# Interleaving the first two units of a down projection over shared weight tiles

## The chip, the cores and the metric

The kernel runs on one core of a Trainium2 chip. The metric is device time in microseconds, the median of three runs. A core has TensorE (PE, with its weight loads shown as PEld), VectorE (DVE), ScalarE (ACT), GpSimd (POOL) and SyncE (SP); here SP issues every transfer.

## The reference

One transformer block over 4096 tokens of width 512, all in float32: causal linear attention, a residual and a layer norm, then a feed-forward network and a second residual and layer norm. The change lies in the last part of the feed-forward network:

```
x = fwht(x * SU_ug) / SCALE
x_up   = x @ W_up.T   * (Wscale_ug[:INTER] * SCALE)      # INTER = 2048
x_gate = x @ W_gate.T * (Wscale_ug[INTER:] * SCALE)
x = silu(x_gate) * x_up
x = fwht(x * SU_dp) / SCALE
x = x @ W_down.T * (Wscale_dp * SCALE)                   # 2048 -> 512: the down projection
x = layernorm(residual + x)
```

The second transform and the scales are folded into W_down ahead of time.

## The kernel before

The kernel goes through its work in stages: attention, output projection, gate/up, down. The gate/up stage has 32 rounds `n` (four blocks `f` of 1024 tokens by eight `p`). It stores its results to DRAM (`hop_d`). The down stage takes them up again as eight units `(f, jp)` of 512 tokens.

Both stages multiply 2 x 2 block matrices with seven products instead of eight. So a unit of the down stage has seven products `s` from 0 to 6. Product `s` multiplies an operand of the unit (activations, or sums of them, from `hop_d`) with weight matrix `s` (from `wdop_d`), and the results are added up in PSUM and on VectorE. `SEQ` names the PSUM bank of each product: a, c, a, b, a, a, b. In the profile these banks are `ps_da`, `ps_dc` and `ps_db`.

Each operand is float32 and is cut into a high and a low part by `hilo`: ScalarE copies it into the high part (L89), and VectorE or GpSimd subtracts (L90). Each multiplication then takes three matmuls (high by high, high by low, low by high). One product of a unit is 48 matmuls of 128 x 256.

The names and lines that matter:
- `h_load(n, s)` loads the operand of unit `n`, product `s`, in four quarters (`hraw`) of 256 KB. `h_split` cuts them into `hah` and `hal`. `h_split_x` does it for the first two operands, into other memory (`hxh`, `hxl`).
- `load_b(s)` loads weight matrix `s` in four quarters (`braw`) of 256 KB. `split_b(s)` cuts them into `wdh`, `wdl` (quarters 0 and 1) and `wdzh`, `wdzl` (quarters 2 and 3), kept in `BW[s]` for all units.
- `hraw` and `braw` share the pool `rp` of 10 buffers: a new load waits until an older quarter has been cut. `hah` and `hal` share 19 buffers.
- `y_load(n)` loads the residual rows of unit `n` as two halves (`yres`). There are two buffers for each half. `acc` (L1035, in the changed file L1034) adds a bank to `yres`. `finish` normalizes a half and stores it to `out`.
- The products of the last round of gate/up (`cc` L882 and L852, `sg` L891, sums `hS` L942) are stored to `hop_d` while the down stage begins.

The list `order` says in which order the products run. Units 0 to 7 run one after the other, with product 0 of each next unit moved ahead of product 5 of the one before:

```
order = [(n, s) for n in range(len(units)) for s in range(7)]
for n in range(1, len(units)):
    order.remove((n, 0))
    order.insert(order.index((n - 1, 5)), (n, 0))
```

During unit 0 every product also cuts one weight matrix and loads another, and the last round of gate/up already prepares the operands of products 0 and 1 and weights 0 to 2. From unit 1 on, only activations are loaded.

The program order is not the final order. The framework's scheduler (`schedule_with_timeline_sim=True`) sets the order of the instructions on each engine, from its own estimate of times. On the chip each engine then runs its list in order, and an instruction that waits holds up all behind it. SP is such a list too.

Of the kernel before, what the change touches and what calls it, by code (L numbers as in the profile page):

```python
# [43 lines left out]
def kernel(  # L44
# [734 lines left out]
    HR, HOP, YN, bank = {}, {}, {}, {}  # L779
    units = [(f, jp) for f in range(4) for jp in range(2)]  # L780

    def h_load(n, s):
        f, jp = units[n]
        HR[n, s] = []
        for qd in range(4):
            raw = rp.tile([128, 2, 256], F32, tag="ar", name="hraw")
            dma(raw, hop_d[f][s, jp, :, 2 * qd:2 * qd + 2])
            HR[n, s].append(raw)

    def load_b(s):  # L790
        RAW["b", s] = []
        for j in range(4):
            x = rp.tile([128, 2, 256], F32, tag="ar", name="braw")
            dma(x, wdop_d[s][:, 2 * j:2 * j + 2])
            RAW["b", s].append(x)
# [13 lines left out]
            ops[l] += [hl[l][:, r] for r in range(4)]  # L809
        BW[s] = ops  # L810

    def h_split_x(s, his, los):
        HOP[0, s] = []
        for qd, raw in enumerate(HR.pop((0, s))):
            hi, lo = (x[qd // 2][:, 2 * (qd % 2):2 * (qd % 2) + 2] for x in (his, los))
            hilo(hi, lo, raw, G if qd == 3 else V)
            HOP[0, s].append((hi, lo))

    with ExitStack() as es:
        pa = es.enter_context(tc.tile_pool(name="g1", bufs=1, reuse_waits="tile"))  # L820

        def utile(name):
            return pa.tile([128, 512], F32, tag="u", name=name, bufs=16)

        def araw(name):
            return rp.tile([128, 2, 2, 128], F32, tag="ar", name=name)

        def ff_front(i):
            y2 = []
            for e in range(2):  # L830
                y = utile("y_nat")
                dma(y, y_d[2 * i + e])
                y2.append(y)
            yield
            yield from front(i, y2, pa, lambda s, n: pgu.tile(s, F32, tag="a", name=n, bufs=4),
                             lambda s, n: pgu.tile(s, F32, tag="a", name=n, bufs=4), (ytile, xtile))

        for s in range(7):
            aload(1, s, araw("A"))
        NS = 32  # L840
        yraw, late_puts = [], []
        fr = None
        for n in range(NS):
            f, p = divmod(n, 8)
            bank, sv, c = {}, {}, {}

            def emit(u, q, x):
                if u == 1:
                    S.activation(x, x, AF.Silu)  # L849
                    c["g", q] = x  # L850
                else:
                    G.tensor_tensor(x, x, c.pop(("g", q)), ALU.mult)  # L852
                    c["h", q] = x

            if n in (1, 2, 4, 5):
                step(fr, 9)
                fr = ff_front(12 + (1, 2, 4, 5).index(n))
            new = {}
            for s, tag in enumerate(SEQ):
                first = SEQ.index(tag) == s  # L860
                wh, wl = AOP.pop((n, s))
                yh, yl = YOPS[s]
                for u in (1, 0):
                    if first:
                        bank[tag, u] = pgu.tile([128, 512], F32, tag=tag, name="ps_" + tag, bufs=4 if tag == "a" else 2)
                    ps = bank[tag, u]
                    i = 0
                    for k in range(2):
                        for w, y in ((wh, yh), (wh, yl), (wl, yh)):
                            T.matmul(ps, w[:, u, k], y[:, k], start=first and i == 0, stop=i == 5,  # L870
                                     skip_group_check=not first)
                            i += 1
                    it = 2 * p + (s >= 4 and s < 6)
                    sc = wsc[:, u, it:it + 1]
                    if s in (0, 2, 4):
                        x = pa.tile([128, 512], F32, tag="sv", name="sv", bufs=6)
                        S.activation(x, ps, AF.Copy, scale=sc)  # L877
                        sv[s, u] = x
                    if s in (1, 4, 6):
                        src, k, q = {1: (ps, 0, 0), 4: (bank.get(("b", u)), 4, 3), 6: (ps, 2, 1)}[s]  # L880
                        x = utile("cc")
                        V.scalar_tensor_tensor(x, src, sc, sv[k, u], ALU.mult, ALU.add)  # L882
                        emit(u, q, x)
                    if s == 5:
                        if u == 1:
                            x = utile("sg")
                            S.activation(x, ps, AF.Silu, scale=sc)
                            c["g", 2] = x
                        else:
                            x = c.pop(("g", 2))  # L890
                            V.scalar_tensor_tensor(x, ps, sc, x, ALU.mult, ALU.mult)  # L891
                            c["h", 2] = x
                if n and s in (1, 2, 3):
                    for _ in range(3):
                        if late_puts:
                            late_puts.pop(0)()
                if n + 1 < NS:
                    asplit(n + 1, s)
                if n + 2 < NS:
                    aload(n + 2, s, araw("A"))  # L900
                if p == 7:
                    if f < 3:
                        new[s] = ysplit(s, yraw[s])
                        if s < 5:
                            yraw.append(yload(f + 1, s + 2))
                    elif s == 0:
                        hx = [xtile([128, 4, 256], F32R, "hxh") for _ in range(2)]
                        hx += [ytile([128, 4, 256], F32R, x) for x in ("hxl", "hxl", "hxh", "hxh", "hxl", "hxl")]
                        h_split_x(0, hx[0:2], hx[2:4])
                        h_load(0, 1)  # L910
                    elif s == 2:
                        split_b(0)
                        load_b(1)
                    elif s == 3:
                        h_split_x(1, hx[4:6], hx[6:8])
                        load_b(2)
                    elif s == 4:
                        split_b(1)
                        h_load(0, 2)
                    elif s == 6:  # L920
                        split_b(2)
                        load_b(3)
                elif n == NS - 2:
                    if s == 4:
                        h_load(0, 0)
                    elif s == 6:
                        load_b(0)
                step(fr)
            if p == 6 and f < 3:
                yraw = [yload(f + 1, 0), yload(f + 1, 1)]  # L930
            YOPS.update(new)
            H = {"A11": c["h", 0], "A12": c["h", 2], "A21": c["h", 1], "A22": c["h", 3]}

            def put(key, f=f, p=p, H=H):
                dma(hop_d[f][WKEY.index(key)].rearrange("j p i t -> p j i t")[:, :, p],
                    H[key].rearrange("p (j t) -> p j t", j=2))

            late_puts = [lambda k=k, put=put: put(k) for k in ("A11", "A12", "A22", "S1", "S3", "S2", "S4")]
            for key, x0, x1, op in (("S1", "A21", "A22", ALU.add), ("S3", "A11", "A21", ALU.subtract),
                                    ("S2", "S3", "A22", ALU.subtract), ("S4", "A12", "S2", ALU.add)):  # L940
                H[key] = utile("h" + key)
                G.tensor_tensor(H[key], H[x0], H[x1], op)  # L942

    with ExitStack() as es:
        pd = es.enter_context(tc.tile_pool(name="d1", bufs=2, reuse_waits="tile"))
        order = [(n, s) for n in range(len(units)) for s in range(7)]
        for n in range(1, len(units)):
            order.remove((n, 0))
            order.insert(order.index((n - 1, 5)), (n, 0))
        def y_load(n):  # L950
# [38 lines left out]
            dma(out[t * 128:(t + 1) * 128], y)  # L989

        y_load(0)
        for idx, (n, s) in enumerate(order):
            if 0 < idx and idx + 1 < len(order):
                h_split(*order[idx + 1])
            if n == 0 and s + 3 < 7:
                split_b(s + 3)
            if 0 < idx and idx + 2 < len(order):
                h_load(*order[idx + 2])
            if n == 0 and s + 4 < 7:
                load_b(s + 4)  # L1000
            if idx > 0:
                for put in late_puts[:3]:
                    put()
                late_puts = late_puts[3:]
            if s == 3 and n + 1 < len(units):
                y_load(n + 1)
            tag = SEQ[s]
            first = SEQ.index(tag) == s
# [98 lines left out]
```

## Time and profile before

| what | value |
|---|---|
| median of three runs | 2345.06 us (2343.75 to 2345.25) |
| time of the profiled execution | 2340.29 us |
| span of the profiled execution | 2338.2 us |
| granted TensorE clock, mean | 0.989 |
| TensorE (PE) busy | 2269.3 us, 97% |
| VectorE busy | 1812.0 us, 77% |
| ScalarE busy | 1401.7 us, 60% |
| GpSimd busy | 1243.7 us, 53% |
| moved by DMA | 484.16 MB, mean 207 GB/s |
| first matmul of the down stage (L1025) | 1984.75 us |
| last matmul of gate/up (L870) starts | 1999.60 us |

Times in the profile count from the start of the span. A busy engine is not at once the bound: what counts is which wait ends last at a place. "Granted clock" is the share of full speed at which TensorE was let run. In a list of waits, "A <- B" means that A stood idle until B was done.

### The profile page before, as it was taken

To read this page: it belongs to the slowest core of one execution; us is meant where nothing else is said; L and a number is where in the kernel's file an instruction comes from. 1 tells how busy PE (TensorE), PEld (TensorE's weight loads), DVE (VectorE), ACT (ScalarE), POOL (GpSimd) and SP (SyncE) were. 2 spreads that over 40 slices of the span, in tenths; PEclk is the share of its full clock that TensorE was granted. 3 is DMA by queue.
4 is the path that set the end of the run, shared out by engine and by line. 5 is a ranking of instruction groups with operands and counts; after the bars stand their busy time and mean duration, and the time that the engine had idled before them with its cause. 6 is when DMAs were issued, how large, how long until landed. Compare 5 with 4: busy or idle time off the path is not lost.

```text
span 2338.2 us, 42338 instructions
## 1 busy us (share of the span) xinstructions
PE 2269.3 (97%) x14432; PEld 2015.0 (86%) x14432; DVE 1812.0 (77%) x2812; ACT 1401.7 (60%) x2483; POOL 1243.7 (53%) x999
## 2 busy tenths in 40 slices
PE   7999999988999999899999999999999999899998
PEld 6999999987899999688878887788878888799998
DVE  7999999988898889678898776676766766665555
ACT  6777777766677777344444466655655655555553
POOL 2455454476654445367888526565565555533332
PEclk9999999999999999899999999999999999899999
DMA  6554555677744445878997977775765657867673
GB/s 186 145 152 146 161 161 155 170 214 218 213 133 129 129 135 142 279 256 269 279 294 253 312 240 217 245 254 187 227 207 188 223 189 212 285 229 249 224 248 128
DMA packets 369528, 484.16 MB, mean 207 GB/s; under 512 B 68670, under 2 KB 224384, under 8 KB 365344
## 3 DMA queue, kind: packets, MB, share of 16 engines
q1 hardware_dynamic: 369312, 481.45, 66.0%
q8 instruction: 114, 1.87, 0.3%
q14 instruction: 102, 0.84, 0.1%
HBM read 282.76 MB, written 156.76 MB: 188 GB/s over the span
## 4 chain that ended last, share of the span: by engine, by line
PE 83%; DVE 6%; DMA 5%; issue 2%; POOL 2%; ACT 1%; SPq 1%; DVEq 0%; POOLq 0%; ACTq 0%
PE ps_wo L737 15%; PE ps_a L870 15%; PE ps_qk L244 13%; PE ps_da L1025 8%; PE ps_b L870 7%; PE ps_num L371 5%; PE ps_db L1025 4%; PE ps_c L870 4%; PE ps_s L294 3%; PE ps_v L197 3%; PE ps_dc L1025 2%; PE ps_sc L337 1%; PE ps_sc L338 1%; PE ps_den L372 1%; DVE x L230 1%
## 5 line engine op out<-in xcount | busy, mean ns | idle before, releaser
L351 POOL TENSOR_SCALAR_AFFINE_SELECT A<-A 64x512 fp32r<-64x512 f32 x256 | 220.4, 861 | 286.9 <-DVE am L347 187.5
L244 PE MATMUL ps_qk<-xh,wh 128*128 128x256 f32 x1280 | 358.9, 280 | 6.3 <-DVE x L230 3.7
L244 PE MATMUL ps_qk<-xl,wh 128*128 128x256 f32 x1280 | 356.9, 279 | 0.6 <-DVE xl L90 0.6
L244 PE MATMUL ps_qk<-xh,wl 128*128 128x256 f32 x1280 | 357.1, 279 | 0.0
L90 DVE TENSOR_TENSOR wol<-A,woh 128x512 fp32r<-128x512 f32 x217 | 231.4, 1071 | 106.9 <-ACT woh L89 92.4
L852 POOL TENSOR_TENSOR cc<-cc 128x512 f32<-128x512 f32 x96 | 149.2, 1556 | 278.8 <-ACT cc L849 169.9
L226 POOL TENSOR_TENSOR sw<-sw,csb 128x512 f32<-128x512 f32 x160 | 219.7, 1374 | 141.9 <-ACT sw L225 133.8
L244 PEld LDWEIGHTS ps_qk<-xh,wh 128*128 128x128 f32 x1280 | 242.5, 189 | 8.0 <-DVE x L230 3.3
L244 PEld LDWEIGHTS ps_qk<-xl,wh 128*128 128x128 f32 x1280 | 241.7, 189 | 2.0 <-DVE xl L90 0.8
L244 PEld LDWEIGHTS ps_qk<-xh,wl 128*128 128x128 f32 x1280 | 241.7, 189 | 0.8
L89 ACT ACTIVATE woh<-A 128x512 fp32r<-128x512 f32 x217 | 135.5, 630 | 129.0 <-PE ps_b L870 75.2
L89 ACT ACTIVATE hah<-hraw 128x512 fp32r<-128x512 f32 x216 | 134.8, 630 | 129.5 <-PE ps_da L1025 68.1
L870 PE MATMUL ps_a<-yol,woh 128*128 128x512 f32 x512 | 202.5, 395 | 0.0
L90 POOL TENSOR_TENSOR hal<-hraw,hah 128x512 fp32r<-128x512 f32 x77 | 101.5, 1319 | 189.1 <-PE ps_da L1025 73.1
L870 PE MATMUL ps_a<-yoh,woh 128*128 128x512 f32 x512 | 201.9, 396 | 0.0
L870 PE MATMUL ps_a<-yoh,wol 128*128 128x512 f32 x512 | 199.4, 396 | 0.0
L90 DVE TENSOR_TENSOR hal<-hraw,hah 128x512 fp32r<-128x512 f32 x139 | 102.3, 744 | 111.7 <-PE ps_da L1025 45.7
L737 PE MATMUL ps_wo<-wh,oh 128*128 128x512 f32 x448 | 178.6, 399 | 2.8 <-ACT oh L89 2.8
L737 PE MATMUL ps_wo<-wh,ol 128*128 128x512 f32 x448 | 178.6, 399 | 0.0
L737 PE MATMUL ps_wo<-wl,oh 128*128 128x512 f32 x448 | 178.0, 397 | 0.0
L231 ACT ACTIVATE sw<-x,neg 128x512 f32<-128x512 f32 x160 | 115.5, 722 | 78.0 <-DVE x L230 75.9
L877 ACT ACTIVATE sv<-ps_a,wsc 128x512 f32<-128x512 f32 x192 | 127.2, 680 | 39.6 <-PE ps_a L870 39.5
(256 smaller groups left out, 7290.2 us busy)
## 6 DMA issues: line engine op xcount, KB each, us to landing
hraw<-hop_d SPq DMA_DIRECT2D x224, 256.0 KB
vd<-vhl SPq DMA_DIRECT2D x128, 256.0 KB
num_d<-num SPq DMA_DIRECT2D x128, 256.0 KB
rb<-rec_d SPq DMA_DIRECT2D x128, 256.0 KB
hop_d<-hS SPq DMA_DIRECT2D x128, 256.0 KB
nt<-num_d SPq DMA_DIRECT2D x31, 1024.0 KB
A<-in_wug_dram SPq DMA_DIRECT2D x93, 256.0 KB
hop_d<-cc SPq DMA_DIRECT2D x64, 256.0 KB
```

Of the source, the lines that this page charges most:

```text
L89: S.activation(hi, src, AF.Copy)
L90: eng.tensor_tensor(lo, src, hi.bitcast(F32), ALU.subtract)
L226: G.tensor_tensor(sw, sw, sinb, ALU.mult)
L231: S.activation(sw, x1, AF.Exp, bias=neg1)
L244: T.matmul(ps[:, j], W[key][wa][:, k * 128:(k + 1) * 128], B[xa][:, k], start=i == 0, stop=i == 11)
L351: G.affine_select(ah, ah.bitcast(F32), pattern=[[0, 8], [1, 64]], compare_op=ALU.is_ge, fill=0.0, base=0, channel_multiplier=-1)
L371: T.matmul(ps[:, c2], l, r, start=i == 0, stop=i == len(ops) - 1)
L737: T.matmul(ps, l[:, h], r, start=i == 0, stop=i == 47)
L852: G.tensor_tensor(x, x, c.pop(("g", q)), ALU.mult)
L870: T.matmul(ps, w[:, u, k], y[:, k], start=first and i == 0, stop=i == 5, skip_group_check=not first)
L877: S.activation(x, ps, AF.Copy, scale=sc)
L1025: T.matmul(ps[:, j], ops[qd][al][:, r, js], BW[s][bl][ip], start=first and i == 0, stop=i >= 45 or last and i == 23, skip_group_check=True)
```

## The change

Units 0 and 1 take turns: (0,0), (1,0), (0,1), (1,1) and so on to (0,6), (1,6), so that each weight matrix is used twice in a row when it is new. One weight matrix is then cut and one loaded for two products, not for one. Unit 2 starts after (1,6) with all its products in their order; from unit 3 on, the order is the old one.

The preparation in the last round of gate/up changes with it: it loads and cuts the operand of (1,0), in place of (0,1), loads that of (0,1), in place of (0,2), no longer cuts weight 2 and no longer loads weight 3. The residual rows of units 0 and 1 are both loaded at the start, those of unit 2 at (1,6).

```diff
--- before.py
+++ after.py
@@ -809,12 +809,12 @@
             ops[l] += [hl[l][:, r] for r in range(4)]
         BW[s] = ops
 
-    def h_split_x(s, his, los):
-        HOP[0, s] = []
-        for qd, raw in enumerate(HR.pop((0, s))):
+    def h_split_x(n, his, los):
+        HOP[n, 0] = []
+        for qd, raw in enumerate(HR.pop((n, 0))):
             hi, lo = (x[qd // 2][:, 2 * (qd % 2):2 * (qd % 2) + 2] for x in (his, los))
             hilo(hi, lo, raw, G if qd == 3 else V)
-            HOP[0, s].append((hi, lo))
+            HOP[n, 0].append((hi, lo))
 
     with ExitStack() as es:
         pa = es.enter_context(tc.tile_pool(name="g1", bufs=1, reuse_waits="tile"))
@@ -907,7 +907,7 @@
                         hx = [xtile([128, 4, 256], F32R, "hxh") for _ in range(2)]
                         hx += [ytile([128, 4, 256], F32R, x) for x in ("hxl", "hxl", "hxh", "hxh", "hxl", "hxl")]
                         h_split_x(0, hx[0:2], hx[2:4])
-                        h_load(0, 1)
+                        h_load(1, 0)
                     elif s == 2:
                         split_b(0)
                         load_b(1)
@@ -916,10 +916,7 @@
                         load_b(2)
                     elif s == 4:
                         split_b(1)
-                        h_load(0, 2)
-                    elif s == 6:
-                        split_b(2)
-                        load_b(3)
+                        h_load(0, 1)
                 elif n == NS - 2:
                     if s == 4:
                         h_load(0, 0)
@@ -943,8 +940,9 @@
 
     with ExitStack() as es:
         pd = es.enter_context(tc.tile_pool(name="d1", bufs=2, reuse_waits="tile"))
-        order = [(n, s) for n in range(len(units)) for s in range(7)]
-        for n in range(1, len(units)):
+        order = [(n, s) for s in range(7) for n in range(2)]
+        order += [(n, s) for n in range(2, len(units)) for s in range(7)]
+        for n in range(3, len(units)):
             order.remove((n, 0))
             order.insert(order.index((n - 1, 5)), (n, 0))
         def y_load(n):
@@ -989,20 +987,21 @@
             dma(out[t * 128:(t + 1) * 128], y)
 
         y_load(0)
+        y_load(1)
         for idx, (n, s) in enumerate(order):
             if 0 < idx and idx + 1 < len(order):
                 h_split(*order[idx + 1])
-            if n == 0 and s + 3 < 7:
-                split_b(s + 3)
+            if n == 0 and s + 2 < 7:
+                split_b(s + 2)
             if 0 < idx and idx + 2 < len(order):
                 h_load(*order[idx + 2])
-            if n == 0 and s + 4 < 7:
-                load_b(s + 4)
+            if n == 1 and s + 3 < 7:
+                load_b(s + 3)
             if idx > 0:
                 for put in late_puts[:3]:
                     put()
                 late_puts = late_puts[3:]
-            if s == 3 and n + 1 < len(units):
+            if n and s == (6 if n == 1 else 3) and n + 1 < len(units):
                 y_load(n + 1)
             tag = SEQ[s]
             first = SEQ.index(tag) == s
```

## The prediction

> **What bounds the kernel now.** I read the page first, then the chain of waits, the waits of TensorE, and the windows and timelines around the one hole that these showed.
>
> ```profile
> span 2338.2 us, 42338 instructions
> PE 2269.3 (97%) x14432; PEld 2015.0 (86%) x14432; DVE 1812.0 (77%) x2812; ACT 1401.7 (60%) x2483; POOL 1243.7 (53%) x999
> PEclk9999999999999999899999999999999999899999
> ```
>
> TensorE is busy for 97% of the span and runs at full clock but for two of the forty slices. So only a hole in TensorE's row, or a slow clock behind one, can give time. The second of those slices (2280 to 2338) is the tail, which the change leaves alone. The change lies at about 2000 us; TensorE's waits there:
>
> ```profile
> PE ps_da L1025 <- ACT hah L89: 10.5, 1, 10.5
> PE ps_da L1025 <- DVE hal L90: 0.6, 1, 0.6
> ```
>
> One wait of 10.5 us, for a ScalarE split. What ScalarE did (start, duration, idle time before it and its cause):
>
> ```profile
> 2009.27 0.63 ACT L89 ACTIVATE wdh<-braw 128x512 fp32r<-128x512 f32 x1 [6.89 <-DMA braw<-wdop_d]
> 2010.51 0.63 ACT L89 ACTIVATE wdh<-braw 128x512 fp32r<-128x512 f32 x1 [0.61 <-DMA braw<-wdop_d]
> 2015.55 0.63 ACT L89 ACTIVATE wdzh<-braw 128x512 fp32r<-128x512 f32 x1 [4.41 <-DMA braw<-wdop_d]
> 2016.74 0.63 ACT L89 ACTIVATE wdzh<-braw 128x512 fp32r<-128x512 f32 x1 [0.56 <-DMA braw<-wdop_d]
> 2017.28 3.22 ACT L89 ACTIVATE hah<-hraw 128x512 fp32r<-128x512 f32 x6
> ```
>
> The activations (`hah`) that TensorE wants at 2007 stand in ScalarE's queue behind four splits of weight matrix 5, which is needed three products later. Its quarters 2 and 3 load into the buffers that quarters 0 and 1 leave, so two transfers follow each other. The chain of waits prices a transfer of 256 KB, early and late in the hole:
>
> ```profile
> 1986.37 3.05 DMA braw<-wdop_d
> 1997.37 3.34 DMA braw<-wdop_d
> 2005.91 4.58 DMA braw<-wdop_d
> 2012.51 4.21 DMA braw<-wdop_d
> ```
>
> The clock by 4 us windows (last columns: granted clock, DMA share, GB/s):
>
> ```profile
> 2004.00:2008.00 4.00, 3.48 (x30) 3.28 (x28) 1.56 (x3) 0.00 (x0) 2.88 (x3) 1.00 0.86 273
> 2008.00:2012.00 4.00, 0.00 (x0) 0.00 (x0) 1.71 (x2) 1.26 (x2) 3.78 (x3) 0.90 0.86 275
> 2012.00:2016.00 4.00, 0.00 (x0) 0.00 (x0) 1.08 (x2) 0.45 (x1) 0.00 (x0) 0.50 0.94 314
> 2020.00:2024.00 4.00, 4.00 (x21) 4.00 (x21) 4.00 (x3) 2.41 (x5) 3.63 (x3) 0.50 1.02 377
> 2024.00:2028.00 4.00, 4.00 (x32) 4.00 (x32) 4.00 (x6) 2.67 (x6) 1.74 (x1) 0.89 0.99 354
> ```
>
> Mixing 1.00 and 0.50 in these rows, the clock halved at 2011.2, 3.8 us after the last matmul, and came back at 2024.9, 5.5 us after matmuls ran without a break (2019.33).
>
> **What the hole costs.** The next product could have begun at 2007.3 and ended 5.7 us later (48 matmuls take 5.71 us in the chain), at 2013.0. It ended at 2027.3 (first `ps_db` matmul 2027.36). The loss is 14.3 us: 10.6 until its first matmul, 1.1 more until the third (0.6 of it the wait for `hal`), 2.5 from matmuls every 0.21 us and not 0.119.
>
> **Traffic.** In unit 0 every product (5.7 us) needs four loads of activations and four of weights: 2.1 MB, 368 GB/s. The fastest row above moved 377 at a DMA share of 1.02. After the change, two products (11.4 us) share four weight loads: 12 loads, 3.1 MB, 276 GB/s, a rate that the trace holds with room. ScalarE, VectorE and GpSimd likewise split 12 quarters per 11.4 us instead of 16. I cost the later pairs at nothing; the cover is TensorE's own 11.4 us per pair. In the old order TensorE had no wait from 2019.4 to the tail, though DMA moved 338 GB/s from 2020 to 2040.
>
> **The new order, step by step.** Instructions, matmuls and transfers are the same in number; only their order changes, up to the third unit; I read it from the changed program, engine by engine, with what each instruction waits for. Until 1991 the queues agree, so times are on the trace's clock. (u,s) is unit u, product s.
>
> 1. TensorE now runs (0,0), (1,0), then (0,1), (1,1). The last gate/up matmul still ends at 2000, and (1,0) at 2007.4, where the second product ended before. Then (0,1) is wanted.
> 2. ScalarE's queue now has the splits of weight 3 ahead of `hah` of (0,1): the same queue jam, with weight 3 in place of 5, and earlier. Its quarter 0 is issued once VectorE has split quarter 2 of weight 2: about 1994.15. Landing 3.3 us later, 1997.45; `wdh` 0.63, `wdl` 0.69: 1998.8; quarter 2 is issued at 1998.9. Quarter 1 (issued 1996.5, behind a GpSimd split) lands at 1999.8; its `wdl` stands behind `cc` and `sg` on VectorE (0.74 each) and a SiLU on ScalarE: 2001.4. Quarter 3 is issued at 2001.5. With 3.9 us (between 3.34 early and 4.58 late) it lands at 2005.4; its split ends at 2006.0. `hah` of (0,1), quarters 0 and 1: 2006.6 and 2007.1, in time.
> 3. The new wait. On VectorE the `yres` addition of (1,0) stands ahead of every `hal` of (0,1). It needs unit 1's `y` rows, whose loads stand on SP behind quarter 3 and a `hraw` load, issued at 2004.4 and 2004.8; landing 2008.7 at 3.9 us. Addition 0.69 (2009.4), `hal` 0.8 (such splits take 0.68 to 1.78 us in the trace, the most when GpSimd works beside them): 2010.2. TensorE, idle since two matmuls after 2007.4, goes on then: a gap of 2.6 us. Behind that addition wait all VectorE splits, for them TensorE, and on SP the loads that want their buffers.
> 4. GpSimd: `cc` (2003.4), two `hS` of 1.25 (2005.9), `wdzl` of quarter 3 (2007.3), two more `hS` (2009.9), then `hal` of quarter 1: 2011.3; TensorE wants it at 2011.6. No loss.
> 5. `hah` of quarter 2 reuses memory of the gate/up stage and waits for the store of S2 (issued 2008.7, landed 2012.6 at 3.9 us): `hah` 2013.2, `hal` 2013.9, wanted at 2013.0. Gap 0.9 us. Quarter 3 is in time.
> 6. (0,1) ends at 2016.5 where 2013.0 was possible: 3.5 us lost. The loads of (0,2) are issued by about 2014, and TensorE wants them from 2022; each later product has more slack.
> 7. Units 1 to 2: `y` of unit 2 takes unit 0's buffer and waits for its output store. Counting from the end of (0,6): normalized by 7.2 us, stored by 11.3, `y` loaded by 16, added by 18; TensorE asks for it at 20.8, since product (2,3) has been put ahead of (2,2). 2.8 us spare: nothing. From unit 3 the order is the old one.
>
> Gain: 14.3 − 3.5 = 10.8 us. The profiled execution took 2340.29 us (span 2338.2 and 2.1 around it), so it would become 2329.5. It lies 4.8 us (0.2%) below the median of 2345.06; on the median I predict **2334.3**.
>
> **Bounds, and two rules weighed.** *Transfer time.* Every load in the jam lies between 3.05 and 4.7 us (quarter 2 of weight 5, issued 2010.84, used 2015.55). The Trainium skill (DMA: Bandwidth & Descriptors, Anatomy of one DMA) gives 2.0 us plus bytes over 436 GB/s, for another queue: 2.6 us for 256 KB. By it, step 3's gap shrinks to some 1.3 us and step 5's goes: 1.5 lost, gain 12.8. The rows are of this queue under this traffic, so I take them. At 4.7 throughout, the chain of step 2 ends at 2007.6, `y` at 2011.8, the first `hal` at 2013.2: a gap of 5.6 us.
> *Clock.* The row: halved 3.8 us after the last matmul. The skill (TensorE: Matmul & The Clock Gate) speaks against this change: it allows no gap over about 3 us (Why this matters for your kernels), and its window runs free of the kernel (What's actually happening). My 2.6 us gap passes by both; at 3.3 us the rule would halve the clock and the row would not. A halving costs 2.5 us by the row of this trace, 3.0 with the slow first two matmuls. So the loss lies between 0 (all covered) and 5.7 + 3.0 = 8.7 us; I take 3.5.
>
> **The rivals.**
> - *Slow landings and a cold clock* (0.22): the 5.6 us gap and the clock loss, 8.7 us in all. Gain 5.6: 2339.5. For it: 4.2 to 4.7 us was what transfers took at 2005 to 2016. Against: the chain's first half lies before 2002, where they took 3.0 to 3.4.
> - *The hole only moves* (0.11): the change doesn't do what it says, since weight 3 blocks the queue as weight 5 did. The loss is again 13 to 14 us: 2345. For it: the queue order in step 2. Against: weight 3 starts 11 us earlier than weight 5 did (1994.15 against 2005.4).
> - *Slower* (0.08): the jam comes back at weights 4, 5 and 6, whose splits stand before `hah` in ScalarE's queue too. Each such hole would cost 14.3 us; two give 2334.3 + 28.6, about 2363. It decides once these holes sum to over 10.8 us. Against: weight 4 should be split by 2026, and (1,2), behind it, is wanted from 2030.
>
> **How the numbers follow.** The likeliest case, a small gap at full clock, has 0.59; faster than before by over 0.2% (4.7 us, about what a measurement of this kernel can tell from no change) are it and most of the second case (0.18 of 0.22): 0.77. Within 0.2%: 0.15. Slower: 0.08. The range goes from no loss at all (2330.8, less a microsecond of spread: 2329.5) to just past the second case: 2341.0.
>
> **What would show it.** Right: TensorE's longest wait near 2000 falls from 10.5 us to about 3, for `hal` from VectorE rather than `hah`; the granted clock stays at 1.00 there; the `yres` addition of unit 1 ends near 2009; all later matmuls start about 11 us earlier. Wrong: a clock row of 0.5, a wait of ScalarE for `braw` that reaches past 2008, a new TensorE wait in the paired products, or one for `yres` at the third unit.

## The result, and the profile after

The changed kernel takes 2340.89 us (median of 20 runs, 2339.28 to 2348.49) where the kernel before takes 2345.99 in the same series (20 runs, 2342.94 to 2350.96). The ratio is 0.9982, with a 95% interval of 0.9975 to 0.9988: about 4.2 us gained, between 2.8 and 5.9. Forecast were 10.8 us. The sign was right, the size less than half.

The profiled execution has nearly the same span as that of before, so the page alone shows no gain:

```profile
span 2338.0 us, 42331 instructions
PE 2269.2 (97%) x14432; PEld 2015.3 (86%) x14432; DVE 1813.9 (78%) x2811; ACT 1401.8 (60%) x2483; POOL 1250.3 (53%) x1000
PEclk9999999999999999899999999999999999999999
```

The two executions differ ahead of the change: the last gate/up matmul starts at 2004.17 here and at 1999.60 in the profile of before, and the work up to there was not edited but for the last round of gate/up. Compared matmul by matmul, the whole difference is there by 1590 us. Such differences are the spread from run to run (8 to 9 us in either series). Stages must therefore be compared from a common point. From that matmul to the last recorded matmul pass 327.14 us, against 331.93 before: 4.8 us gained, in agreement with the ratio.

A ledger of that stretch tells more. Matmuls of the down stage follow each other every 0.1189 us; what a stretch takes beyond its count times 0.1189 is lost. Before, 14.3 us are lost at the hole, and 1.9 in the tail, which is the same in every trace to 0.1 us and left out below. After the change 8.1 us are lost at the same place, and 1.3 at the third unit: 9.4 in all.

TensorE's waits after the change (total, times, longest):

```profile
PE ps_dc L1024 <- DVE hal L90: 3.4, 1, 3.4
PE ps_dc L1024 <- ACT hah L89: 2.0, 1, 2.0
PE ps_da L1024 <- DVE yres L1034: 1.9, 2, 1.1
```

The wait of 10.5 us has become one of 2.0 for `hah` and one of 3.4 for `hal`, with two matmuls between them; of the third row, 1.06 us are new (0.88 is the tail's). ScalarE's timeline shows why `hah` is late (start, duration, idle before and its cause):

```profile
2004.14 0.64 ACT L89 ACTIVATE wdh<-braw 128x512 fp32r<-128x512 f32 x1 [3.79 <-DMA braw<-wdop_d]
...
2008.85 0.63 ACT L89 ACTIVATE wdzh<-braw 128x512 fp32r<-128x512 f32 x1 [1.45 <-DMA braw<-wdop_d]
2012.97 0.63 ACT L89 ACTIVATE wdzh<-braw 128x512 fp32r<-128x512 f32 x1 [3.48 <-DMA braw<-wdop_d]
2013.50 1.14 ACT L89 ACTIVATE hah<-hraw 128x512 fp32r<-128x512 f32 x2
```

It is the picture of before with weight 3 in place of weight 5: four splits, three of them (shown) waiting for transfers, and behind them the activations that TensorE wanted at 2012.2. On VectorE the same queue holds up the end of gate/up (the `wdl` stands ahead of `cc` and `sg`), and the residual addition of unit 1 stands ahead of every `hal`:

```profile
2004.81 0.69 DVE L90 TENSOR_TENSOR wdl<-braw,wdh 128x512 fp32r<-128x512 f32 x1 [5.84 <-ACT wdh L89]
2016.60 0.69 DVE L1034 TENSOR_TENSOR yres<-ps_da,yres 128x512 f32<-128x512 f32 x1 [5.22 <-DMA yres<-y_d]
2017.21 0.86 DVE L90 TENSOR_TENSOR hal<-hraw,hah 128x512 fp32r<-128x512 f32 x1
```

And the clock was halved again. The windows (TensorE's busy time first; granted clock, DMA share and GB/s last):

```profile
2012.00:2016.00 4.00, 0.68 (x4) 0.30 (x2) 0.00 (x0) 1.67 (x3) 3.48 (x3) 1.00 0.79 234
2016.00:2020.00 4.00, 1.88 (x9) 1.89 (x10) 1.47 (x2) 0.08 (x1) 3.11 (x3) 0.52 0.94 303
2020.00:2024.00 4.00, 4.00 (x24) 4.00 (x24) 3.07 (x3) 4.00 (x8) 2.85 (x2) 0.63 1.00 280
```

Of the 8.1 us, 5.9 are the gap and 2.2 the matmuls at half clock that follow it.

### The profile page after: what moved, and what is told of

Read it like the earlier page. It is cut to its first block, busy times and chain, and to the rows that moved or that the text cites. A ratio compares the mean times of both kernels' runs of the same rounds, so it can differ in the third digit from the quotient of the medians.

```text
span 2338.0 us, 42331 instructions
## 1 busy us (share of the span) xinstructions
PE 2269.2 (97%) x14432; PEld 2015.3 (86%) x14432; DVE 1813.9 (78%) x2811; ACT 1401.8 (60%) x2483; POOL 1250.3 (53%) x1000
## 4 chain that ended last, share of the span: by engine, by line
PE 81%; DVE 7%; DMA 6%; issue 2%; POOL 2%; ACT 1%; SPq 1%; DVEq 0%; POOLq 0%; ACTq 0%
PE ps_wo L737 15%; PE ps_a L870 14%; PE ps_qk L244 13%; PE ps_b L870 7%; PE ps_da L1024 7%; PE ps_num L371 5%; PE ps_db L1024 4%; PE ps_c L870 4%; PE ps_s L294 3%; PE ps_v L197 3%; PE ps_dc L1024 2%; PE ps_sc L337 1%; PE ps_den L372 1%; PE ps_sc L338 1%; DVE x L230 1%
## 5 line engine op out<-in xcount | busy, mean ns | idle before, releaser
L90 POOL TENSOR_TENSOR hal<-hraw,hah 128x512 fp32r<-128x512 f32 x78 | 106.4, 1368 | 178.0 <-PE ps_da L1024 73.5
L90 DVE TENSOR_TENSOR hal<-hraw,hah 128x512 fp32r<-128x512 f32 x138 | 108.1, 791 | 94.2 <-PE ps_da L1024 37.8
```

What stands on the lines that cost most here:

```text
L90: eng.tensor_tensor(lo, src, hi.bitcast(F32), ALU.subtract)
```

## The experiments

All ratios are to the kernel before, from runs on the same chip. The ledger gives what one profiled execution lost (us, tail left out).

| kernel | lost at the first hole | lost later | ratio, 95% interval |
|---|---|---|---|
| before | 14.3 | 0 | 1 |
| the change | 8.1 | 1.3 | 0.9982 (0.9975 to 0.9988) |
| the change again | 7.5 | 4.3 | 0.9983 (0.9975 to 0.9991) |
| weights 3 to 6 later | 1.9 | 13.8 | 0.9978 (0.9970 to 0.9987) |
| y halves exchanged | 6.4 | 3.7 | 0.9972 (0.9961 to 0.9983) |
| useless matmuls in the gap | 7.8 | 5.8 | 0.9980 (0.9972 to 0.9987) |
| old order, late weights | 9.3 | 2.7 | 0.9986 (0.9979 to 0.9993) |
| unit 0 ended first | 6.3 | 0.6 | 0.9975 (0.9965 to 0.9985) |
| pairs, old prefetch | 10.0 | 1.7 | 0.9991 (0.9985 to 0.9998) |
| three repairs | 0.4 | 6.8 | 0.9965 (0.9952 to 0.9977) |
| three repairs again | 0.4 | 5.8 | 0.9957 (0.9943 to 0.9972) |
| three repairs, other boundary | 0.4 | 5.7 | 0.9954 (0.9942 to 0.9966) |

The profiled executions of "weights 3 to 6 later" and "useless matmuls" were 3 to 4 us slower than the medians of their kernels (spans of 2342.7 and 2343.1 us), so their later losses are probably on the high side. In the first of them the trace lost 15.7 us in all, more than the kernel before, although the ratio says 5 us faster. One trace gives the place of a loss; only the ratios give the size. The intervals of the single edits overlap with that of the change, so none of them alone is shown to be faster or slower than it. In the row of the useless matmuls, the 3.8 us of useless work count as lost.

**Which half of the change gives the gain?** The change does two things: it pairs the products (with both units' residual rows loaded at the start), and it takes up weights one product later. First the later weights alone, in the old order:

```
-            if n == 0 and s + 3 < 7:
-                split_b(s + 3)
+            if n == 0 and s + 2 < 7:
+                split_b(s + 2)
...
-            if n == 0 and s + 4 < 7:
-                load_b(s + 4)
+            if n == 0 and s + 3 < 7:
+                load_b(s + 3)
```

(and without the split of 2 and the load of 3 in the last gate/up round).

> The old order of products (no interleaving) with the change's later prefetch alone: weight s+2 is split and weight s+3 is loaded in each product of unit 0, and the last gate/up round no longer splits 2 and loads 3. Theory A (the place of the queue jam decides, the interleaving little): weight 4 stands in the jam, earlier than weight 5 did; hole 6.5 to 7.5 us instead of 10.5, halved clock, loss about 10 us against 14.3 of the old order, so 4 us faster than it, near to the change itself. Theory D (interleaving is what gives the gain): no faster than the old order, or slower through new waits of TensorE for weights in products 3 to 6 of unit 0.

It gained 3.3 us. ScalarE's splits in the jam are now those of weight 4:

```profile
2009.90 0.63 ACT L89 ACTIVATE wdh<-braw 128x512 fp32r<-128x512 f32 x1 [5.73 <-DMA braw<-wdop_d]
2010.75 0.64 ACT L89 ACTIVATE wdh<-braw 128x512 fp32r<-128x512 f32 x1 [0.21 <-DMA braw<-wdop_d]
2015.17 0.63 ACT L89 ACTIVATE wdzh<-braw 128x512 fp32r<-128x512 f32 x1 [3.78 <-DMA braw<-wdop_d]
2017.92 0.63 ACT L89 ACTIVATE wdzh<-braw 128x512 fp32r<-128x512 f32 x1 [2.12 <-DMA braw<-wdop_d]
2018.45 1.13 ACT L89 ACTIVATE hah<-hraw 128x512 fp32r<-128x512 f32 x2
```

The hole costs 9.3 us, as theory A had it, and the small new waits (2.7 us lost before products 4 and 5 of unit 0, where theory D had looked for them) don't eat the gain.

Then the pairs alone, with the old prefetch (`split_b(s + 3)`, `load_b(s + 4)`, and the split of 2 and the load of 3 in the last round again).

> The changed order of products with the old order's prefetch: weights 2 and 3 are taken up in the last gate/up round, weight s+3 is split and s+4 loaded in the pairs. Weight 4 then stands in the jam. With the experiment before it (old order, late prefetch: about 9.3 us lost at the hole) this is the other half of the change alone. Theory A (the place of the jam decides): a hole of 6 to 7 us and a halved clock, loss 9 to 10 us, 3 to 5 us faster than the old order. Theory D (the interleaving is the gain): loss 8 us or less, as in the change.

10.0 us at the hole, weight 4 in the jam again, a gain of 2.1 us (0.5 to 3.5). Theory D fails in both. Each half moves the jam from weight 5 to weight 4, the two together to weight 3. With each step it begins earlier and costs less: the first split of the jam starts 9.7 us after the last gate/up matmul before, 5.0 and 4.9 us after it with one half, and together with it in the change. The size fell a little below what theory A gave, because 1.7 us went at the third unit.

**What holds the gap of the change open?** Weight 3 was taken out of the jam, the pairs kept. Against the words of the expectation below, the edit takes up weights 4 to 6 one product later too:

```
-            if n == 0 and s + 2 < 7:
-                split_b(s + 2)
+            if n == 0 and s == 0:
+                split_b(2)
+            if n == 1 and 0 < s < 5:
+                split_b(s + 2)
...
-            if n == 1 and s + 3 < 7:
-                load_b(s + 3)
+            if n == 0 and 0 < s < 5:
+                load_b(s + 2)
```

> The changed kernel with weight matrix 3 loaded and split two products later, so that none of its four splits stands ahead of the first activations of (0,1) in ScalarE's and VectorE's queues; all else as in the change. Theory A (those splits, waiting for their transfers, hold up the tail of gate/up, the S stores, the y loads and the activations): TensorE's gap after (1,0) falls from 5.4 us to about 1.7 (VectorE's yres addition of (1,0) and one hal are still ahead), no halved clock, loss at this place 8.1 -> about 1.7 us, about 6 us faster than the change, 11 us faster than the old order. Theory B (the y loads, not the splits, are the bound): gap stays above 4 us with a halved clock, gain over the change below 2 us. Theory C (too much traffic in the paired products): a new TensorE wait for weight 3 at (0,3).

At the hole theory A was right to a few tenths: a gap of 1.64 us, full clock, 1.9 us lost. So the splits of weight 3 held the gap open. But the kernel is 5.2 us faster than before and not 11. In the trace the gain was given back later, in a form that none of the three theories had:

```profile
PE ps_da L1026 <- DVE yres L1036: 9.8, 3, 5.0
```

The 5.0 us lie at 2064: weight 6 was issued at 2049.67, behind eight activation loads that waited for buffers; it took 6.3 us until its first split, and behind its splits came `hah`, `hal` and the additions that free the PSUM bank. Another 3.89 us lie at the third unit. As weight 6 was itself moved by this edit, the jam at 2064 may be of the edit's own making; what a closed hole uncovers by itself is read below, from the kernel with three repairs.

Next the residual halves of unit 1 exchanged buffers, which puts the addition of (1,0) behind three `hal`; the jam stayed:

```
-                y = (pd.tile([128, 2, 512], F32, tag="yn", name="yres") if half else
+                y = (pd.tile([128, 2, 512], F32, tag="yn", name="yres") if half != (n == 1) else
                      xtile([128, 2, 512], F32, "yres"))
```

> The changed kernel with the two residual halves of unit 1 exchanging their buffers, which puts the yres addition of (1,0) on VectorE behind three hal of (0,1); the splits of weight 3 stay where the change has them. Theory A (everything behind the splits of weight 3 is late, the y rows are only the latest): hah of (0,1) still comes at about 2 us after (1,0), GpSimd's hal of quarter 1 and the store of S2 are late next; the one gap of 5.4 us becomes several below 3 us, the clock stays at 1.00, loss 8.1 -> about 6 us, 2 us faster than the change. Theory B (the wait for the y rows is the cause): loss about 2 us, 6 us faster than the change.

Theory A comes nearer: 6.4 us lost at the hole where it said 6, and GpSimd is late next. By the ratios it is 2.3 us ahead of the change, but the intervals overlap. Theory B fails: without the wait for y the gap remains, in three parts: 0.65 us for `hah`, 0.23 and 3.27 for `hal`. The clock did not stay at 1.00, as theory A had it: it was halved from 2017.84 to 2021.25, behind the gap of 3.27.

```profile
PE ps_dc L1024 <- POOL hal L90: 3.3, 1, 3.3
PE ps_dc L1024 <- ACT hah L89: 0.6, 1, 0.6
```

**What halves the clock?** 32 useless matmuls, 3.8 us, were put into the gap after (1,0):

```
+            if idx == 2:
+                for ip in range(8):
+                    for wl in (0, 1) * 2:
+                        T.matmul(ps[:, ip % 2], BW[0][wl][ip][:, 0:128], BW[1][wl][ip], start=ip + wl == 0,
+                                 stop=ip + wl == 8, skip_group_check=True)
```

> The changed kernel with 32 extra matmuls of 128 x 256 on weight tiles after (1,0), into the bank that (0,1) then starts afresh: 3.8 us of useless work inside the 5.4 us gap. If the gap of TensorE halves the clock and this costs 2.5 us: the granted clock stays at 1.00 there, (0,1) runs at 0.119 us per matmul, and the kernel is about 2 us faster than the change although it does more. If the clock has another cause: halved as before, and the time the same or up to 1 us longer.

The clock was halved again, so the forecast of the first theory missed, but not for the reason of the second: TensorE was left with a gap of 2.25 us (2017.14 to 2019.39), the only idle time there, and behind it the clock was halved from 2020.5 to 2023.9. The loss at the place is 7.8 us, the time that of the change. A gap far shorter than the 3.8 us of the prediction's row is enough. In the kernel with exchanged halves one of 1.94 us, later on (2063.2 to 2065.15, a wait for `hah`), was too:

```profile
2062.00:2064.00 2.00, 1.21 (x11) 1.00 (x9) 2.00 (x2) 0.20 (x1) 1.85 (x2) 1.00 0.86 263
2064.00:2066.00 2.00, 0.85 (x6) 0.89 (x7) 1.97 (x4) 1.35 (x3) 0.89 (x1) 0.91 0.95 341
2066.00:2068.00 2.00, 2.00 (x11) 2.00 (x11) 2.00 (x3) 0.86 (x2) 0.83 (x2) 0.50 1.03 384
2068.00:2070.00 2.00, 2.00 (x15) 2.00 (x14) 1.01 (x3) 0.49 (x2) 0.86 (x1) 0.74 0.95 332
```

The rows put the half clock at 2065.64 to 2069.04: it began after TensorE had gone on, and lasted 3.4 us.

**What opens at the third unit?** Only the last paired products were put in another order, so that unit 0 ends 5.7 us earlier:

```
-        order = [(n, s) for s in range(7) for n in range(2)]
+        order = [(n, s) for s in range(5) for n in range(2)] + [(0, 5), (0, 6), (1, 5), (1, 6)]
```

> The changed kernel with only the last four paired products in another order: (0,5), (0,6), (1,5), (1,6), so that unit 0 ends one product earlier and its buffer comes free 5.7 us earlier for the y rows of unit 2. If the wait for those rows at unit 2 is a chain of store and load behind the end of unit 0: it goes (1.3 us of loss in the trace of the change, 5.7 in the two experiments whose first hole was smaller), the first hole stays at about 8 us; 1 to 3 us faster than the change. If it is the busy queue and not the end of unit 0: the wait stays, the same time as the change.

The loss there fell to 0.6 us (1.3 and 4.3 in the two traces of the change). The ratio is 1.6 to 1.9 us better than the change's, with intervals that overlap, and the first hole was smaller in this trace too (6.3 us). The place is what the forecast said; with one trace, and a loss that varies from 1.3 to 4.3 without the edit, the size is not shown.

**Together, and what is left.** Weight 3 loaded at (0,1) and split at (1,1), weights 4 to 6 as in the change; halves exchanged and unit 0 ended first by the edits above:

```
-            if n == 0 and s + 2 < 7:
+            if (n, s) in ((0, 0), (1, 1)) or n == 0 and 1 < s < 5:
                 split_b(s + 2)
...
-            if n == 1 and s + 3 < 7:
-                load_b(s + 3)
+            if (n, s) == (0, 1) or n == 1 and 0 < s < 4:
+                load_b(s + 2 + n)
```

> The changed kernel with all three repairs: weight 3 loaded at (0,1) and split at (1,1), weights 4 to 6 as in the change, the residual halves of unit 1 exchanged, and unit 0 ended first. If jam, y wait and unit boundary are all there is: first hole below 1 us of loss, no halved clock, no wait at unit 2, at most 2 us lost in all against 14.3 in the old order; 12 us faster than that, 7 faster than the change. If the transfers of the pairs have no room (12 loads of 256 KB per 11.4 us): a wait of TensorE of 2 us or more between 2035 and 2070, for hah or for weights, and at most 7 us faster than the old order.

2336.67 us, 8.2 faster than before. The first hole is gone (0.4 us lost). What remains is the wait for `hah` in the pairs that the rival forecast, beside one at the third unit (start, duration, idle before):

```profile
2060.35 0.35 PE L1024 MATMUL ps_da<-wdh,hah 128*128 128x256 f32 x1 [2.98 <-ACT hah L89]
2096.79 0.55 PE L1024 MATMUL ps_da<-wdh,hah 128*128 128x256 f32 x1 [1.99 <-DVE yres L1034]
```

The first stands behind two activation loads in a row, with a split between them, through a ring of 10 buffers (from the chain of waits, start and length):

```profile
2047.46 4.70 DMA hraw<-hop_d
2052.16 1.77 DVE hal L90
...
2053.95 5.61 DMA hraw<-hop_d
```

DMA moved 215 to 245 GB/s there, at a share of 0.80 to 0.83 (rows in the last section), less than the 384 GB/s at 1.03 of a row above. So it is the loads' standing in line for buffers, and not a full queue, that fits this wait; a larger ring was not tried.

Last, the same kernel again, and one with products of unit 2 moved between those of unit 1.

> The kernel with the three repairs once more, for the spread of what is left: first hole below 1 us of loss, and 3 to 7 us of loss between 2040 and 2100, for activations whose raw buffers come free late or for the y rows of unit 2. If this remainder was chance in one profile: below 2 us.

> The kernel with the three repairs, and the products around the end of units 0 and 1 in the order (0,5), (0,6), (1,5), (2,0), (2,1), (1,6), (2,3), (2,2): unit 2's second product in bank a comes 28.5 us after the end of (0,6) instead of 22.8, and the stores of units 0 and 1 no longer stand side by side. If the wait at unit 2 is the time from the end of unit 0 through store and load (store 6.8, load 2.8 us in the trace of the kernel with three repairs): it goes, 3.5 us of loss with its halved clock, and the kernel comes to about 2333, 3 us faster than with three repairs alone. If the transfers are simply too many there, another wait of 2 us or more takes its place. The wait for hah near 2057 (3.2 us) stays by both.

The remainder comes back in the repeat: 6.8 and 5.8 us. There it lies nearly whole near 2060 (a wait of 3.2 us and a halved clock) and nothing at the third unit, so the moved boundary, at 0.9954 beside 0.9957, is not shown to help. Its wait at the third unit is gone (0.1 us lost), but near 2057 it loses 5.6, where the repeat loses 5.3. Both are 10 to 11 us faster than the kernel before in these runs, about 6 faster than the change.

## Why the prediction was wrong, point by point

The mechanism was right and the sizes were not. The prediction took 3.5 us off the gain for what the new order loses; the trace of the change lost 9.4. Of the 5.9 us between them, 2.4 are longer gaps at the hole (5.9 for 3.5), 2.2 the halved clock behind them, which the text put at nothing, and 1.3 the third unit, put at nothing as well. The step that failed first is the transfer times in steps 2 and 3.

- *What bounds the kernel, and where:* right. The loss of 14.3 us is one queue jam, and the change moves it.
- *Steps 1 and 2, the order of the queues:* right, as far as the rows above show it. Step 2 failed in its **transfer times**. Quarter 0 of weight 3 was taken to land 3.3 us after issue; issued at 1998.22, it let ScalarE go on at 2004.14, 5.9 us later. That was no chance of one execution: in the five traces with weight 3 in the jam this time is 5.0 to 5.9 us. Quarter 2 took 3.3, quarter 3 4.8 (3.9 in the text; 2.8 to 4.8 in the five traces). So `hah` came 2 us after TensorE wanted it, where the text had "in time".
- *Step 3, the new wait for the `yres` addition:* the right wait, wrongly sized: a gap of 5.4 us of idle time, not 2.6. Shifted by the 4.57 us between the traces, the y loads were to be issued at 2009.0 and 2009.4; they went from 2011.22 on, behind a `hraw` load that waited for its buffer. The addition began 5.4 us after the first of these issues, where the text had 4.3; it is 5.4 to 5.5 in the four traces where the addition waits for them. SP's rows for steps 2 and 3 (start, duration of the issue):

```profile
1998.22 0.33 SPq L58 DMA_DIRECT2D braw<-wdop_d  x1
2011.22 1.02 SPq L58 DMA_DIRECT2D yres<-y_d  x2
```

- *Step 5:* the store of S2 let `hah` of quarter 2 go at 2019.92, 2.7 us later than forecast. It made no gap of its own; TensorE ran at half clock until 2022.96 and so asked later.
- *The clock:* put at nothing because the forecast gap was short; the gap of 5.4 us halved it by either bound of the text, and that cost 2.2 us. The bounds failed too: the gap was held to be safe below 3 to 3.8 us, and the experiments show the clock halved behind 1.94, 1.99 and 2.25 us. Even the forecast gap of 2.6 us was not safe.
- *Step 7, the third unit:* "2.8 us spare: nothing" failed. TensorE asked 20.6 us after the end of (0,6), as forecast (20.8), and unit 0's stores went out from 7.2 on, as forecast. But the loads of unit 2's rows, behind those stores and, on SP, behind two loads of unit 3 that wait for unit 1's store, were issued at 14.7 instead of 11.3, and took some 6 us instead of 4.7, while two units' stores, residual rows and activations shared the queue (DMA share 0.93 to 1.07). The wait was 1.06 us in this trace, 2.5 in the repeat, with a halved clock there.
- *The later pairs "cost at nothing":* true of the change, where TensorE comes so late that the loads keep up. With the hole repaired, about 3 us of waiting appear near 2060 in all three such traces (2.8 to 3.2); so the cover in the change was probably that lateness, and not the 11.4 us per pair.
- *The rivals:* "slow landings and a cold clock" was what happened: a gap of 5.6 us and 8.7 us lost were forecast there, 5.4 and 8.1 measured. That the numbers are so near is partly luck: the text took 4.7 us for every transfer, and they took 5.9, 3.3 and 4.8. The text preferred the short times because the chain's first half lay before 2002, where its rows showed 3.0 to 3.4. But the trace of before has a slow load there too, which the text overlooked. It is quarter 1 of weight 4, issued just behind two loads of residual rows, and ScalarE waited for it until 4.7 us after its issue:

```profile
1995.46 0.43 SPq L58 DMA_DIRECT2D braw<-wdop_d  x1
2000.18 0.63 ACT L89 ACTIVATE wdh<-braw 128x512 fp32r<-128x512 f32 x1 [2.01 <-DMA braw<-wdop_d]
```

In the change, four activation loads and four stores stand just ahead of weight 3. "The hole only moves" was right in kind. "Slower" did not come.
- *A reading of the page:* the two slow slices of the clock are 935 to 994 us and 1987 to 2046, not one of them the tail. The second is the hole itself; the first lies in an earlier stage that the change leaves alone. The forecast does not rest on it. Nor does it on the low end of the range, where 2330.8 less a microsecond is 2329.8 and not 2329.5.

What stays open: how much of the 5.9 us of quarter 0 is waiting behind other transfers. No run measured that transfer alone.

## What to carry to other kernels

A transfer's time is not one number: loads of the same 256 KB took 3.0 to 5.9 us around the hole. When an edit changes what stands beside a load in the queue, take the slow row for the forecast, not the one nearest in time. A prefetch that stands ahead of the needed work in an in-order queue costs its landing time: ask first whether it can stand behind. When a hole closes, everything that it had covered (loads through a small ring, stores at the end of a unit) is next in line, so a repair is worth the hole less what lay hidden in it: closing 14.3 us gave 8 to 11.

## What the runs showed of the hardware that was not expected

The length of TensorE's gap alone doesn't decide on the halved clock. A gap of 2.98 us left it at 1.00, and one of 1.99 us in the same execution halved it (kernel with three repairs):

```profile
2056.00:2060.00 4.00, 1.36 (x12) 1.16 (x10) 4.00 (x4) 1.59 (x3) 2.45 (x2) 1.00 0.80 245
2060.00:2064.00 4.00, 3.65 (x31) 3.68 (x32) 3.97 (x6) 2.72 (x5) 1.29 (x1) 1.00 0.83 215
2092.00:2096.00 4.00, 2.80 (x24) 2.59 (x22) 0.05 (x1) 2.31 (x5) 1.30 (x1) 1.00 0.63 224
2096.00:2100.00 4.00, 3.21 (x15) 3.24 (x16) 2.44 (x4) 0.23 (x1) 0.39 (x1) 0.60 0.86 200
```

The halved stretches last 3.41 us or a multiple: once that behind the gaps of 1.94, 1.99 and 2.25 us, twice (6.8) in the change, three times (10.2) in the pairs with the old prefetch, four times (13.7) before, from 2011.22 to 2024.88. Their starts, too, lie whole multiples of it apart, across stages: in the change the clock is halved at 940.93 and again at 2016.13, which is 1075.2 us or 315 times 3.413. That fits a clock which is set once per fixed window by how busy the last one was, as the Trainium skill describes it (TensorE: Matmul & The Clock Gate, What's actually happening: a free-running window of 3413 ns).

Laid on that grid, the windows of all twelve traces agree, from the hole to the third unit. Full clock stayed after a window with up to 1.86 us of idle TensorE in it (54%), and was halved after every window with 1.94 us or more (57%). The gap of 1.99 us lay in one window; that of 2.98 us was split into 1.86 and 1.12. The way back asks for more: a halved window with 0.23 us of idle time was followed by full clock, those with 0.58 us or more by another halved one. The page's advice of no gap over about 3 us (Why this matters for your kernels) is too generous here. These bounds are for this stream of matmuls: in earlier stages halved stretches follow windows with as little as 0.7 us of idle time by the same count.

Each halving costs half of a window's matmuls, about 1.7 us, and can begin when TensorE is already busy again (1.1 us after the gap of 2.25 us had ended), where nothing else is wrong.
